# Two more token groups by seven products, three bands and statistics ahead, in a fused attention and convolution kernel

## The chip, the cores and the metric

The kernel runs on one core of a Trainium2 chip. The metric is the device time of one execution in microseconds. The engines are named as the profile names them: PE multiplies matrices, DVE, ACT and POOL work elementwise, and SP does nothing here but issue DMAs. Each engine takes its instructions in the order in which the kernel wrote them; instructions of different engines wait for each other by semaphores.

## The reference, cut to what matters

Two layers on an image batch x of shape (2, 56, 56, 384), all in float32. Layer 0 is neighbourhood attention and then an MLP; layer 1 is a projection to 768 channels, a 3x3 depthwise convolution, four exponential scans (both ways along rows and along columns), a projection back, and an MLP.

```python
# layer 0
x = x + neighborhood_attention(layer_norm(x), ...)            # result: x1
y = layer_norm(x, ln2_g, ln2_b)
x = x + (gelu(y @ w1 + b1) @ w2 + b2)                         # result: x2; w1 384x1536, w2 1536x384
# layer 1
p = _layernorm(x, n1_g, n1_b) @ w_in + b_in                   # 384 -> 768
local = conv_general_dilated(p, k_conv, ..., feature_group_count=768)   # 3x3 depthwise
lr, rl = _ema_scan(local, axis=2), _ema_scan(local, axis=2, reverse=True)
tb, bt = _ema_scan(local, axis=1), _ema_scan(local, axis=1, reverse=True)
mixed = _layernorm(0.25 * (lr + rl + tb + bt) + local, on_g, on_b)
x = x + (mixed @ w_out + b_out)
x = x + (gelu(_layernorm(x, n2_g, n2_b) @ w1 + b1) @ w2 + b2)
```

## The kernel before

**Stages.** The attention comes first (about the first 690 us). Its result x1 goes to DRAM (`x1f`). Then `passes` makes two passes over the 6272 tokens, in tiles of 128 tokens. The first pass runs the MLP of layer 0 and the projection to 768 channels; the second runs the projection back and the MLP of layer 1. Between them stands the convolution with its scans, which DVE computes beside the matrix products of both passes.

**Groups of the first pass.** `sizes` makes 13 groups: group 0 of one tile, groups 1 to 12 of four tiles (512 tokens). In each, group g's MLP runs (12 blocks of `hidden`, then `tokens`), and with it the previous group, held in `waiting`, is normalized and projected (`project_in`), which stores its 768 channels to DRAM as `p_d`. The next group's input `x_next` is loaded by SP (`load_group`, the tile `xa`) at the end of the group before. Its layer norm needs mean and variance per token: DVE takes them (`norm_next.add`: one bn_stats and one bn_aggr per tile), POOL takes the power -1/2, and ACT applies them.

**Groups by seven.** In the groups of `EARLY` (here 1 and 2) both MLP products are made from 2x2 blocks with seven block products in place of eight (`hidden_by_seven`, `tokens_by_seven`; L1580 and L1669 are their matmuls). Group `EARLY.stop` (here 3) is half early: `hidden` by seven, `tokens` plain. The early groups turn the next group's input on DVE (L1178), plain groups on PE (L269). The scratch tiles of the early groups lie in the pool `tp`, with one buffer per name. In the half early group `begin_convolution` frees that pool and opens the pool `cp` for the convolution in its place.

`hidden_by_seven` runs three rounds u = 0, 1, 2. In each round it calls `next(measuring)` twice, and there the generator `both()` puts in the work for the neighbouring groups, two of the twelve steps m for each call. I call these places slots: slot 1 and slot 2 of round u. In DVE's order the work of slot 2 stands in front of the addition L1627 of that round (PE's bank `z` plus the tile `u2`), and the work of slot 1 of round u + 1 stands between L1627 and the addition L1599 of round u (in `finish`). PE needs L1627 done before it adds to the same bank `z` in `finish`. ACT waits for L1599 with a gelu, and behind that gelu stands its copy L1619, which frees the bank that PE needs next.

**The convolution's plan.** `Beside` is a planner. Its jobs are `Band` (one band of image rows, one block of 128 channels: eight taps L1302, two scans L1248 and L1252) and `Columns` (the scans along columns). `BANDS` cuts the 56 rows of each image; a band is queued once `project_in` has covered its rows and the one below. After each piece of PE work the code calls `beside.go(worth, own)`: `worth` is the PE time by the planner's account (2.6 for one block `hidden`, 7.8 for one tile of `tokens`), `own` the DVE time of the group's own statistics, and DVE work of `rate * worth - own` is written out. `rate` is 1.06, and 0.98 from the last group on. Before the last group, `beside.until((0, NI - 1))` writes out whatever is left of image 0. In groups from `EARLY.stop` on, DVE takes the statistics of `x_next` at step m = 2, and those of `waiting`'s last tile at step m = 1.

Of the kernel before, what the change touches and what calls it, by code (L numbers as in the profile page):

```python
# [42 lines left out]
P = 128  # L43
# [4 lines left out]
NT = 4  # L48
# [15 lines left out]
    ((0, 19), (19, 28), (28, 37), (37, 47), (47, 56)),  # L64
# [49 lines left out]
class Beside:  # L114
# [3 lines left out]
    def __init__(self):  # L118
        self.jobs, self.due, self.finished, self.idle = [], 0.0, set(), True
        self.late, self.rate = [], 1.06  # L120
        self.steps = self.run()
# [38 lines left out]
    def go(self, worth, own=0.0):  # L160
        self.due += self.rate * worth - own
        while self.due > 0.0:
            step = self.step()
            if step is None:
                self.due = 0.0
            else:
                self.due -= step
# [9 lines left out]
def block_kernel(ctx: ExitStack, tc: tile.TileContext, ins: dict, out: bass.AP):  # L177
# [464 lines left out]
    EARLY = range(1, 3)  # L642
# [449 lines left out]
    def passes(xs, xn, w1, w2, between=lambda ps: None):  # L1092
# [164 lines left out]
        class Band:  # L1257
# [6 lines left out]
            def load(self):  # L1264
# [4 lines left out]
                self.pt = half("pt", "in")  # L1269
# [53 lines left out]
        class Columns:  # L1323
# [9 lines left out]
            def load(self):  # L1333
                if not self.loaded:
                    self.loaded = True
                    self.loc = [half("loc", "in") for h in range(2)]
                    for h in range(2):
                        nc.sync.dma_start(out=flat(self.loc[h]), in_=self.rows(loc_d, h))
# [163 lines left out]
        def project_in(g, hT, between=lambda: None, at=1):  # L1502
# [15 lines left out]
            while bands and bands[0][0] * T1 + min(bands[0][2] + 1, H) * W <= t0 + groups[g][1] * P:  # L1518
                b, lo, hi = bands.pop(0)
                last = [j for j in beside.jobs if isinstance(j, Columns) and not j.loaded][-2:]  # L1520
                beside.jobs = [j for j in beside.jobs if j not in last]
                beside.jobs += [Band(b, m, lo, hi) for m in range(NI)] + last
                if hi == H:
                    beside.jobs += [Columns(b, m) for m in range(NI)]

# [201 lines left out]

        ln2, n1 = ("L0_conv_ln2_g", "L0_conv_ln2_b"), ("L1_conv_n1_g", "L1_conv_n1_b")
# [8 lines left out]
        for g, (t0, n) in enumerate(groups):  # L1737
            def begin_convolution():
# [6 lines left out]
                decay = flat(decay)  # L1745
                ps_y = bctx.enter_context(tc.tile_pool(name="psy", bufs=1, space=PSUM))
# [9 lines left out]
            if g == last:  # L1756
# [3 lines left out]
                beside.rate = 0.98  # L1760
            if g < last:
                x_next, n_next = xs.pop(g + 1), groups[g + 1][1]
                norm_next = Norm(sm)
# [22 lines left out]
            def behind(m):  # L1786

                nonlocal xn_next
                if g < last:
# [7 lines left out]
                    if g >= EARLY.stop and m == 2:  # L1797
                        for k in range(n_next):
                            norm_next.add(k, [x_next[:, k, :]])
                        norm_next.close_by_pool(n_next)  # L1800
# [8 lines left out]
            def both():  # L1809
                for m in range(NHID):  # L1810
# [4 lines left out]
                    if m % 2 == 1:  # L1815
                        yield
# [23 lines left out]
            else:  # L1840
                for m in range(NHID):
# [6 lines left out]
                    own = STATS if m == 1 else n * STATS if m == 2 else 0.0  # L1848
# [260 lines left out]
```

## Time and profile before

| what | us |
|---|---|
| three runs | 2565.36, 2565.64, 2573.49; median 2565.64 |
| the profiled execution, its own time | 2573.64 |
| its span, first to last instruction | 2571.8 |
| PE busy in the span | 2545.4 |
| DVE busy in the span | 1973.7 |
| group 2 (by seven), first matmul 758.54 to the next group's 832.55 | 74.01 |
| group 3 (half early), from 832.55 | 79.76 |
| group 4 (with the preparation of w_out), from 912.31 | 85.54 |
| groups 5, 6, 7, ... (plain), from 997.85 | 79.93 or 79.94 each |
| first pass ends (group 12's tokens) | about 1639 |

The span is cut at the first matmul of each group's `hidden`. Start times are microseconds from the span's start. A row of the timeline gives start, duration, engine, line, operation, the tile written and those read, shapes, and in brackets how long the engine sat idle before it and what ended that. A matmul in float32 stands as two rows. "SPq" is SP issuing a DMA. In a table of windows, "busy (x)" is busy time and the number of instructions.

### The profile page before, as it was taken

Reading aid. Unit: us, or ns where it says so; the run is one execution under the profiler, and the core shown is the slowest. Engines: PE = TensorE matmul, PEld = TensorE weight load, DVE = VectorE, ACT = ScalarE, POOL = GpSimd, SP = SyncE. Lnnn points to the kernel's source line nnn. Section 1 sums busy time; section 2 is a strip of 40 time slices with the busy share of each in tenths; the row PEclk is TensorE's granted clock in tenths of the full one; section 3 lists DMA queues with packets and bytes.
Section 4 is the critical chain, followed back from the end, with each engine's and each line's share of the span. In section 5 each row is a group of like instructions: output and inputs, shape, how many; then the busy total and the mean of one; then the engine's idle time right before and its main releaser. Section 6 shows DMA issues by size and latency. Waiting matters only on the chain. (4 is left out here: it accounts for less than half of the span.)

```text
span 2571.8 us, 41605 instructions
## 1 busy us (share of the span) xinstructions
PE 2545.4 (99%) x16438; PEld 1695.7 (66%) x16438; DVE 1973.7 (77%) x3785; ACT 1115.9 (43%) x2030; POOL 560.9 (22%) x610
## 2 busy tenths in 40 slices
PE   9999999999999999999999999999999999999999
PEld 5666666666688645554455555555568888888888
DVE  3888878887544299967999958988887877878861
ACT  4656555555333444344454443333762233233222
POOL 0111111111443011101110011011123333333332
PEclk9999999999999999999999999999999999999999
DMA  6432454225511256655675655777781333333210
GB/s 210 161 100 87 151 190 153 88 85 191 158 43 38 79 147 173 167 132 149 178 273 191 183 174 162 239 208 191 187 213 24 74 74 74 74 74 74 47 28 21
DMA packets 162159, 338.50 MB, mean 132 GB/s; under 512 B 12086, under 2 KB 113952, under 8 KB 159648
## 3 DMA queue, kind: packets, MB, share of 16 engines
q1 hardware_dynamic: 128064, 251.18, 29.1%
q0 software_dynamic: 28944, 57.81, 13.7%
q10 hardware_dynamic: 4944, 26.74, 3.1%
q8 instruction: 131, 2.15, 0.3%
q14 instruction: 76, 0.62, 0.1%
HBM read 171.91 MB, written 134.88 MB: 119 GB/s over the span
## 5 line engine op out<-in xcount | busy, mean ns | idle before, releaser
L1302 DVE SCALAR_TENSOR_TENSOR loc<-pt,taps,loc 128x495 f32<-128x495 f32 (+13 forms) x432 | 397.8, 921 | 25.2 <-ACT loc L1285 9.4
L1195 PE MATMUL mm<-hT,w 128*128 128x512 f32 x864 | 378.6, 593 | 0.6 <-ACT hT L272 0.6
L1195 PEld LDWEIGHTS mm<-hT,w 128*128 128x128 f32 x864 | 161.6, 190 | 193.8 <-issue 185.2
L571 ACT ACTIVATE pts<-pts 119x448 f32<-119x448 f32 (+5 forms) x396 | 210.8, 573 | 110.4 <-DVE pts L561 101.5
L561 DVE TENSOR_TENSOR pts<-sc,bias 119x448 f32<-119x448 f32 (+5 forms) x396 | 219.0, 615 | 45.7 <-PE sc L550 45.4
L1213 PE MATMUL y<-w,hid 128*128 128x384 f32 x648 | 213.6, 486 | 0.2 <-ACT y L1223 0.2
L1213 PE MATMUL y_end<-w,hid 128*128 128x384 f32 x648 | 213.4, 486 | 0.0
L404 PE MATMUL ps<-hT,wqkv 128*128 128x448 f32 x504 | 207.7, 557 | 2.1 <-ACT vs L449 1.5
L1448 DVE STREAM_TRANSPOSE turned<-mx 32x192 f32<-32x192 f32 x528 | 194.8, 369 | 6.9
L1178 DVE STREAM_TRANSPOSE hT<-xn 32x96 f32<-32x96 f32 x656 | 176.8, 270 | 26.0 <-ACT xn L255 17.6
L1206 ACT ACTIVATE hid<-mm,chan 128x512 f32<-128x512 f32 x144 | 98.5, 686 | 185.4 <-PE mm L1195 185.4
L1213 PEld LDWEIGHTS y_end<-w,hid 128*128 128x128 f32 x648 | 122.7, 190 | 84.5
L1213 PEld LDWEIGHTS y<-w,hid 128*128 128x128 f32 x648 | 122.3, 190 | 84.3 <-ACT y L1223 0.8
L1195 PE MATMUL mm<-hT,w_in 128*128 128x512 f32 x396 | 171.9, 593 | 0.6 <-DVE hid_u L1599 0.6
L404 PEld LDWEIGHTS ps<-hT,wqkv 128*128 128x128 f32 x504 | 92.5, 192 | 86.1 <-issue 76.0
L1195 PEld LDWEIGHTS mm<-hT,w_in 128*128 128x128 f32 x396 | 75.1, 190 | 94.9 <-issue 88.8
L1321 POOL DMA_DIRECT2D mix_d<-both x54 | 52.2, 966 | 350.6 <-ACT both L1317 213.4
L227 POOL TENSOR_TENSOR rs<-rs,mhalf 128x4 f32<-128x4 f32 (+4 forms) x56 | 53.8, 960 | 331.1 <-DVE rs L224 321.2
L550 PEld LDWEIGHTS sc<-qT,kT 32*100 32x100 f32 (+3 forms) x3168 | 87.8, 169 | 46.4 <-DVE sum L580 7.6
L590 PE MATMUL o<-pts,vt 100*32 100x112 f32 (+3 forms) x3168 | 116.6, 264 | 0.8 <-ACT pts L571 0.8
L620 PE MATMUL ps<-wproj,og 128*128 128x384 f32 x294 | 107.0, 504 | 2.8 <-DVE og L533 2.1
L550 PE MATMUL sc<-qT,kT 32*100 32x112 f32 (+3 forms) x3168 | 106.5, 268 | 3.1 <-DVE pts L561 3.1
(197 smaller groups left out, 4649.5 us busy)
## 6 DMA issues: line engine op xcount, KB each, us to landing
loc<-loc_d SPq DMA_DIRECT2D x24, 784.0 KB
xa<-x_d SPq DMA_DIRECT2D x24, 768.0 KB
xa<-rows POOLq DMA_DIRECT2D x24, 768.0 KB, 8.6
bias<-in_bias_t ACTq DMA_DIRECT2D x13, 1344.0 KB
p_d<-mx SPq DMA_DIRECT2D x11, 1536.0 KB
mx<-mix_d SPq DMA_DIRECT2D x11, 1536.0 KB
v_d<-vs SPq DMA_DIRECT2D x49, 192.0 KB
xr<-in_x SPq DMA_DIRECT2D x49, 192.0 KB
```

What stands on the lines that cost most here:

```text
L404: nc.tensor.matmul(ps, lhsT=wqkv[:, c, m * P : (m + 1) * P], rhs=hT[:, c, half_of(n)], start=c == 0, stop=c == NC - 1,)
L550: nc.tensor.matmul(sc[i // 2][: w.keys, i % 2, q : q + TT], lhsT=kT[d, hg, w.keys_at + r * w.kc : w.keys_at + (r + w.rows) * w.kc], rhs=qT ...
L561: nc.vector.tensor_tensor(self.pts[:n, h : h + 2, lo:hi, :], sc[half][:n, :, at * TT : (at + hi - lo) * TT].rearrange("p h (c q) -> p h c ...
L571: nc.scalar.activation(t, t, AF.Exp)
L590: nc.tensor.matmul(o[i * HD : (i + 1) * HD, self.slot, :TT], lhsT=w.vt[:n, c, h * HD : (h + 1) * HD], rhs=self.pts[:n, i, c, :], start=c = ...
L620: nc.tensor.matmul(ps, lhsT=ogs[t // 7][:, c, at : at + P], rhs=wproj[:, c, :], start=c == 0, stop=c == NC - 1,)
L1178: nc.vector.transpose(hT[j : j + HD, :, k * P + i : k * P + i + HD], xn[i : i + HD, k, :].rearrange("p (c q) -> p c q", c=NC)[:, :, j : j ...
L1195: nc.tensor.matmul(ps[:, : n * P], lhsT=w[:, c, m * P : (m + 1) * P], rhs=hT[:, c, : n * P], start=c == 0, stop=c == NC - 1,)
L1206: nc.scalar.activation(t[:, : n * P], ps[:, : n * P], AF.Gelu, bias=col(b1, m))
L1213: nc.tensor.matmul(ps, lhsT=t[:, k * P : (k + 1) * P], rhs=w[:, m, :], start=m == 0 and onto is None, stop=m == len(lhs) - 1, skip_group_c ...
L1302: nc.vector.scalar_tensor_tensor(to, pt[:, lo + dy - self.top : hi + dy - self.top, xt : xt + n], self.tap(dy, dx), to, ALU.mult, ALU.add,)
L1448: nc.vector.transpose(t[j : j + HD].rearrange("p (m c) -> p m c", m=NI)[:, :, i : i + HD], mx[i : i + HD, :, k * P + j : k * P + j + HD],)
```

## The change

Groups 3 and 4 join groups 1 and 2 in `EARLY`; the half early group is now group 5. The convolution therefore begins in group 5, and `begun` keeps the planner from writing out bands before that. The first image has three bands in place of five, and the tiles `pt` and column `loc` get one line more. The planner's list is first in, first out: the lines that kept the last two `Columns` behind newly queued bands are gone. The rates are 1.07 and 1.0.

The statistics of x1 for groups 6 to 12 (28 tiles) are taken in the early groups: the generator `statistics_ahead` loads two tiles at a time into one tile `ahead` of the pool `tp`, and at its next call takes two bn_stats and two bn_aggr of it and issues the next load. It is called at the end of every slot of `both()` for g > 1, so at most six times in a group. After the last pair one DVE instruction, one POOL power of 128x28 and one DVE instruction make scale and shift for all 28 tiles. Groups from `EARLY.stop` on use them through `Ready` and take no statistics of `x_next`.

```diff
 BANDS = (
-    ((0, 19), (19, 28), (28, 37), (37, 47), (47, 56)),
+    ((0, 28), (28, 47), (47, 56)),
     ((0, 18), (18, 36), (36, 45), (45, 56)),
 )
...
-        self.late, self.rate = [], 1.06
+        self.late, self.rate, self.begun = [], 1.07, False
...
     def go(self, worth, own=0.0):
+        if not self.begun:
+            return
         self.due += self.rate * worth - own
...
-    EARLY = range(1, 3)
+    EARLY = range(1, 5)
...
-                last = [j for j in beside.jobs if isinstance(j, Columns) and not j.loaded][-2:]
-                beside.jobs = [j for j in beside.jobs if j not in last]
-                beside.jobs += [Band(b, m, lo, hi) for m in range(NI)] + last
+                beside.jobs += [Band(b, m, lo, hi) for m in range(NI)]
...
+        class Ready(Norm):
+            def __init__(self, g):
+                at = groups[g][0] // P - ready_from
+                self.rs, self.sh = (t[:, at : at + NT] for t in (ready_rs, ready_sh))
+
+        ready_from = groups[EARLY.stop + 1][0] // P
+        n_ready = T2 // P - ready_from
...
+        def statistics_ahead():
+            for k in range(0, n_ready, 2):
+                t = tp.tile([P, 2, C], F32, name="ahead")
+                at = (ready_from + k) * P
+                nc.sync.dma_start(
+                    out=t, in_=x1f[at : at + 2 * P, :].rearrange("(k p) c -> p k c", p=P)
+                )
+                yield
+                for i in range(2):
+                    st = sm.tile([P, 2, 6], F32, name="st")
+                    nc.vector.bn_stats(st[:, 0, :], t[:, i, :])
+                    nc.vector.bn_aggr(ready_mv[:, k + i, :], st[:, :1, :])
+            nc.vector.tensor_scalar(ready_rs, ready_mv[:, :, 1], EPS, 1.0, ALU.add, ALU.mult)
+            nc.gpsimd.tensor_tensor(
+                ready_rs, ready_rs, mhalf[:, :1].to_broadcast([P, n_ready]), ALU.pow
+            )
+            yield
+            nc.vector.scalar_tensor_tensor(
+                ready_sh, ready_mv[:, :, 0], -1.0, ready_rs, ALU.mult, ALU.mult
+            )
...
+                beside.begun = True
...
-                beside.rate = 0.98
+                beside.rate = 1.0
             if g < last:
                 x_next, n_next = xs.pop(g + 1), groups[g + 1][1]
-                norm_next = Norm(sm)
+                norm_next = Norm(sm) if g < EARLY.stop else Ready(g + 1)
...
-                    if g >= EARLY.stop and m == 2:
-                        for k in range(n_next):
-                            norm_next.add(k, [x_next[:, k, :]])
-                        norm_next.close_by_pool(n_next)
...
                     if m % 2 == 1:
+                        if g > 1:
+                            next(statistics, None)
                         yield
...
-                    own = STATS if m == 1 else n * STATS if m == 2 else 0.0
+                    own = STATS if m == 1 else 0.0
```

More of the change, by code (lines that the diff above doesn't have):

```diff
@@ L1268, in load @@
                 self.top, end = max(self.lo - 1, 0), min(self.hi + 1, H)
-                self.pt = half("pt", "in")
+                self.pt = cp.tile([P, HALF + 1, W], F32, name="pt", tag="in")
                 nc.sync.dma_start(
@@ L1335, in load @@
                     self.loaded = True
-                    self.loc = [half("loc", "in") for h in range(2)]
+                    self.loc = [
+                        cp.tile([P, HALF + 1, W], F32, name="loc", tag="in")[:, :HALF] for h in range(2)
+                    ]
                     for h in range(2):
@@ L1519, in project_in @@
                 b, lo, hi = bands.pop(0)
-                last = [j for j in beside.jobs if isinstance(j, Columns) and not j.loaded][-2:]
-                beside.jobs = [j for j in beside.jobs if j not in last]
-                beside.jobs += [Band(b, m, lo, hi) for m in range(NI)] + last
+                beside.jobs += [Band(b, m, lo, hi) for m in range(NI)]
                 if hi == H:
                     beside.jobs += [Columns(b, m) for m in range(NI)]
+        class Ready(Norm):
[4 more added lines that the diff above has]
+        n_ready = T2 // P - ready_from
+        ready_mv = wp.tile([P, n_ready, 2], F32, name="ready_mv")
+        ready_rs, ready_sh = (wp.tile([P, n_ready], F32, name=x) for x in ("ready_rs", "ready_sh"))
+        def statistics_ahead():
[18 more added lines that the diff above has]
+            )
         def store_x2(g, x2):
@@ L1726, in open_banks @@
             return ps_y, ps_u, bank_b, banks_b
+        statistics = statistics_ahead()
         ln2, n1 = ("L0_conv_ln2_g", "L0_conv_ln2_b"), ("L1_conv_n1_g", "L1_conv_n1_b")
```

## The prediction

> **What bounds the kernel now.** I read the page first, then a table of windows cut at the groups of the first pass, then the timeline of the first round of an early group, then the waits by length. The page:
>
> ```profile
> PE 2545.4 (99%) x16438; PEld 1695.7 (66%) x16438; DVE 1973.7 (77%) x3785; ACT 1115.9 (43%) x2030; POOL 560.9 (22%) x610
> ...
> PE   9999999999999999999999999999999999999999
> ```
>
> PE is never free, so an instruction less on PE shortens the run by its duration and a wait of PE lengthens it by its length. What the groups cost shows in the windows (length, then busy time of PE, PEld, DVE, ACT, POOL):
>
> ```profile
> 758.54:832.55 74.01, 73.18 (x350) 60.26 (x349) 29.93 (x95) 29.28 (x56) 22.59 (x23) 1.00 0.19 54
> 832.55:912.31 79.76, 78.46 (x292) 52.64 (x291) 30.89 (x45) 31.93 (x61) 5.16 (x6) 1.00 0.31 95
> 912.31:997.85 85.54, 85.54 (x241) 41.30 (x240) 80.68 (x80) 34.99 (x51) 12.55 (x10) 1.00 0.62 165
> 997.85:1077.79 79.94, 79.94 (x230) 41.29 (x229) 74.79 (x112) 33.73 (x55) 12.56 (x13) 1.00 0.64 160
> 1397.53:1477.46 79.93, 79.93 (x229) 41.28 (x228) 77.79 (x77) 34.61 (x50) 9.36 (x9) 1.00 0.59 167
> ```
>
> These are groups 2 (by seven), 3 (half early), 4, 5 and 10 (plain). The plain groups have PE busy throughout. The early group is shorter, but its PE lacks 0.8 us. The timeline shows why, in the first round of group 3, which starts at 832.55:
>
> ```profile
> 833.98 0.36 SPq L648 DMA_DIRECT2D xa<-x_d  x1
> ...
> 839.25 0.56 DVE L219 BATCH_NORM_STATS2 st<-xa 128x6 f32<-128x384 f32 x1 [3.67 <-DMA xa<-x_d]
> ...
> 840.60 0.53 DVE L219 BATCH_NORM_STATS2 st<-xa 128x6 f32<-128x384 f32 x1
> ...
> 842.27 0.68 DVE L1627 TENSOR_TENSOR hid_u<-uz,hid_u 128x512 f32<-128x512 f32 x1
> ...
> 843.09 1.10 PE L1580 MATMUL uz<-xsums,w 128*128 128x256 f32 x4 [0.75 <-DVE hid_u L1627]
> ...
> 845.10 0.69 DVE L1599 TENSOR_TENSOR hid_u<-uz,hid_u 128x512 f32<-128x512 f32 x1 [2.15 <-PE uz L1580]
> ...
> 846.64 0.56 ACT L1619 COPY hid_u<-ub 128x512 f32<-128x512 f32 x1
> ...
> 847.49 1.03 PE L1580 MATMUL ub<-xsums,w_t 128*128 128x256 f32 x4
> ```
>
> DVE waits for xa, takes four statistics (one pair from 839.25 to 840.60: 1.35 us), and only then makes L1627, for which PE waits 0.75 us. Group 2 shows the same, 0.78 us. Next, L1599 starts 2.01 us after that matmul; over a gelu and L1619, which ends at 847.20, it frees the bank that PE takes at 847.49: 0.29 us of slack. So in an early group DVE has no slack in slot 1 and slot 2 of round 0, though it is busy for 40% only.
>
> **What the Trainium skill says.** "DMA: Bandwidth & Descriptors", section on the anatomy of one DMA, fits a DMA as about 2.0 us plus bytes over 436e3 per us, mostly completion; for the 384 KB of one `ahead` load I estimate 2.0 + 0.9 = 2.9 us. That fit is for DMAs that GpSimd issues, ours are SP's. The trace has neighbours:
>
> ```profile
> 299.25 0.33 SPq L609 DMA_DIRECT2D xr<-in_x  x1
> ...
> 301.90 1.00 POOL L614 TENSOR_TENSOR xr<-xr,shift 128x384 f32<-128x384 f32 x1 [3.26 <-DMA xr<-in_x]
> ```
>
> 192 KB are usable 2.65 us after the issue, and 280 KB of `pt` 2.83 us (1211.45 to 1214.28). The 768 KB of xa took 5.27 us beside an equal store. I take 3.0 us for 384 KB. "Perfetto Trace Analysis", section Sequencer Loop, says that an engine's instruction waits for its semaphores in its queue; the trace agrees: the idle DVE leaves L1627 undone while the statistics in front wait for xa. "TensorE: Matmul & The Clock Gate", section on what's happening, puts the clock at half after an idle window of some 3.4 us; the windows above show 1.00 throughout, so no run here shows it yet.
>
> **The change part by part.** *Groups 3 to 6.* Before: 79.76 + 85.54 + 79.94 + 79.93 = 325.2 us. After: groups 3 and 4 as group 2, 2 x 74.01; group 5 half early, 79.76 less 0.75 (it takes no statistics of xa any more, so that wait goes); group 6 with the preparation of w_out, 85.54. Sum 312.6: **12.6 us less**.
>
> *Statistics ahead.* The order in which the changed kernel's instructions stand puts, on DVE, two bn_stats and two bn_aggr of `ahead` in front of L1627 and two more in front of L1599, in every round of groups 2 and 3 but for the very first slot, and up to the third slot of group 4; on SP each `ahead` load waits for DVE, since there is one tile. One slot is thus a trip: load 3.0 us (DVE to SP takes 0.03), pair 1.35. Two trips are 8.8 us, and a round of PE is 9.5, so in steady state they fit. The start of a group doesn't. Group 3, from its start:
> - xa at about 6.1 (before 6.7; the store of x2 now stands behind four loads on SP), four statistics and the small operations 2.85: 8.95.
> - Slot 1: pair (loaded long before), 10.3. Then the load, 13.3.
> - Slot 2: pair, 14.65; L1627, and PE's matmul 0.82 after it (842.27 to 843.09): 15.5, where it was 10.54. **Extra 4.95.**
> - Slot 1 of round 1: load 14.7 to 17.7, pair to 19.05. L1599 would start at 15.5 + 2.01 = 17.5. Late by 1.55, less the slack of 0.29: **extra 1.25.**
> - Slot 1 of round 2: the x2 store shares the wires with the load, about one us; **extra 0.2.**
>
> Group 3: 6.4. Group 4 the same without the last: its third slot ends the 28 tiles, 0.2 for the small operation: 6.3. Group 2: its first slot only loads, so slot 2 adds one pair less 0.15 for what lies between, 1.2; then again 1.2 and 0.2: 2.6. Sum **15.3 us of new waits**. With a load of 2.6 us the sum is about 13, with 3.4 about 18.
>
> *POOL's power of 128x28.* Four columns took 1.0 us (L227). Between 1.0 and, if it goes by columns, 7 us. Its result is wanted by a DVE instruction in front of L1627 of round 1, with about 6 us to spare: I take 0, at most 1.
>
> *PE's clock.* Groups 3 and 4 each get an idle stretch of about 6 us. At worst each costs a window at half speed, 1.7 us; much of it would fall on work that the late L1599 holds up anyway. Taken 0.5, range 0 to 3.
>
> *The convolution in fewer groups.* It had groups 3 to 12, now it has 5 to 12. Adding up what the planner hands out when each kernel is built: before group 12 it has written out 600 us (of its own account) in the old order and 531 in the new, `until` finds nothing left in either, and the queue of bands is then the same. So the plan closes; fewer bands save fixed costs, and the new plan is never empty, where before DVE stood idle 87.4 us for `pt`:
>
> ```profile
> DVE loc L1287 <- DMA pt<-p_d: 87.4, 5, 26.1
> ```
>
> What is to be shown is that DVE keeps the plan. In groups 8 to 10 it was full: 230 us of account took about 224 without the statistics (three windows of 79.93, less 3 x 6.5, plus the 3.7 by which it fell behind), so 0.974 real for one accounted. New: 481 accounted in groups 6 to 11, 468; statistics of x2, 6 x 2.9; w_out 4: 490 us against PE's 6 x 79.93 + 5.6 = 485. DVE falls behind by about 5 us, 1 per group, from 4.5 after group 6's start to about 10 at group 12. How far it was behind there:
>
> ```profile
> 1563.74 0.55 DVE L219 BATCH_NORM_STATS2 st<-xc 128x6 f32<-128x384 f32 x1
> ```
>
> 6.3 us after the group's start 1557.40. The first wait that ends on it is in group 12: PE's second transposes (1573.5) reuse banks that DVE's statistics of the first free (done about 1570.0), 3.9 us of slack. So some 4 more cost about 0.5. Through the planner's new 1.0 the last group of the second pass adds up to 1 to its present wait of 1.7. **Taken 1.5, range 0 to 10.** The longer bands move as many bytes in fewer DMAs, and the prefetch of `pt` is one job ahead: nothing. Fourteen issues on SP of 0.36 us: nothing, SP is idle there. The statistics that leave groups 6 to 12 take no PE time.
>
> Sum: -12.6 + 15.3 + 0.5 + 1.5 = **+4.7 us**. Against the profiled execution's own 2573.6 that is 2578.3; it lies 8.0 above the median of the runs, so on the median 2565.64 it is **2570.3 us**.
>
> **The rivals.** *The trips are hidden.* If the loads land before DVE comes to them, a pair costs only itself: 1.2 in group 2, and 2 x 1.35 less the earlier xa, 2.1, in groups 3 and 4: 5.4 us, and -7.2 in all with nothing for clock and lag, 2558.4. For it: DVE is busy 40% there, xr came in 2.65. Against: one tile, and a load that waits for the pair before.
>
> *DVE loses the plan.* Slower. If DVE falls behind by 2.6 us per group, as it did in group 9 (7.4 us after the start against 4.8 a group earlier), it is 20 behind at group 12, 14 more than before; less the slack of 3.9, PE waits 10 us at the statistics of the mixed rows. Then +13, 2579. It decides from 1.7 per group, where the sum passes +7.7. For it: 80 us of account per group without a pause. Against: group 10, as full, fell behind by 1.1 only.
>
> **How the numbers follow.** The measurement can't tell 0.3% (7.7 us) from no change. Likeliest case 0.60 (2563 to 2577, of which a fifth passes +7.7), hidden trips 0.15, the lost plan 0.25. Faster by over 0.3%: the hidden trips lie at that edge, 0.10 of their 0.15; slower: 0.25 and 0.12 of the likeliest (0.37); within: 0.53. The range 2558 to 2581 takes in the bounds of the waits (13 to 18), the clock and the lag.
>
> **What would show it.** Groups 3 and 4 of the changed profile should last about 80 us, not 74: PE idle about 5.7 us before the z matmul of round 0, ended by L1627's successor, with DVE idle on a DMA of `ahead`; and 1.3 us before the bank of round 1. Group 2 about 76.6, group 5 about 79.0. The last tile's statistic should start about 10 us after group 12's start. I am wrong if groups 3 and 4 last 74 to 76, or if PE waits for DVE in groups 6 to 12.

## The result, and the profile after

The changed kernel takes 2590.92 us (median of five runs, 2588.57 to 2593.11) against 2567.36 us of the kernel before on the same chip: a ratio of 1.0089, 95% interval 1.0074 to 1.0104. It is slower by 23.6 us, and 9.9 us above the end of the range. The profiled execution took 2590.42 us, its span is 2588.6 us.

The page of after, engines and PE's row of the slices:

```profile
PE 2538.1 (98%) x16676; PEld 1736.5 (67%) x16678; DVE 1993.0 (77%) x3783; ACT 1127.4 (44%) x2046; POOL 566.9 (22%) x621
...
PE   9999999999999999999999998999999999999999
```

PE did get less to do (2538.1 us busy, 2545.4 before), but the span grew by 16.8 us. So PE waits more, or runs more slowly, and the page can't tell where. The windows can tell. They are cut as before, at the first matmul of each group's `hidden`: length, busy time of PE, PEld, DVE, ACT, POOL, then PE's granted clock, DMA share and GB/s. Of after:

```profile
750.82:826.67 75.85, 73.45 (x351) 60.26 (x349) 36.45 (x115) 29.45 (x56) 22.59 (x23) 1.00 0.28 84
826.67:908.29 81.62, 75.98 (x349) 62.22 (x349) 37.90 (x119) 29.53 (x56) 22.61 (x23) 0.96 0.27 78
908.29:989.98 81.69, 76.22 (x351) 62.40 (x350) 35.13 (x109) 29.41 (x56) 27.36 (x24) 0.96 0.20 59
989.98:1068.74 78.76, 78.21 (x291) 52.71 (x291) 46.30 (x41) 33.85 (x62) 3.93 (x4) 1.00 0.37 112
1068.74:1154.61 85.87, 85.81 (x241) 41.22 (x240) 80.13 (x55) 35.38 (x48) 6.14 (x7) 1.00 0.72 199
1314.48:1400.23 85.75, 82.12 (x230) 41.90 (x228) 74.49 (x56) 45.70 (x70) 8.03 (x5) 0.98 0.75 257
1560.20:1687.21 127.01, 120.03 (x349) 62.78 (x347) 113.82 (x130) 44.66 (x67) 15.53 (x15) 0.96 0.73 217
```

These are groups 2, 3, 4, 5, 6, 9 and 12. Groups 2 and 3 are longer by 1.8 and 1.9 us, group 4 shorter by 3.9, group 5 by 1.2; group 6 now carries the preparation of w_out that group 4 carried before. Up to there, groups 2 to 6 together are 4.6 us longer, where I had worked out 3.2. The loss stands in two groups that the change seemed hardly to touch: group 9 (79.94 before) and group 12 (115.87 before), with 5.8 and 11.1 us. Of before, the same two groups:

```profile
1317.59:1397.53 79.94, 79.94 (x230) 41.28 (x229) 74.55 (x57) 40.09 (x61) 8.68 (x5) 1.00 0.65 224
1557.40:1673.27 115.87, 115.23 (x349) 60.89 (x347) 103.09 (x121) 45.26 (x68) 16.34 (x13) 1.00 0.69 206
```

In after PE idles 3.6 us in group 9 and is busy 2.2 us longer than before; in group 12 it idles 6.3 us more and is busy 4.8 us longer. The granted clock is below 1.00 in these two windows: 4.8 of group 12's 11.1 us are slow matmuls, not waits.

The attention stage, the same code in all these kernels, ended anywhere from 666.7 to 676.9 us after the span's start in the profiled executions, and was 7.8 us shorter in the profiled run of after than in that of before. From here on I compare the *passes*: from the first `hidden` of group 0 to the first matmul of the last group of the second pass. They took 1874.95 us before and 1899.38 after, 24.4 more, which agrees with the 23.6 of the medians.

### The profile page after: what moved, and what is told of

It is laid out like the page before. It is cut to its first block, busy times and chain, and to the rows that moved or that the text cites. A ratio compares the mean times of both kernels' runs of the same rounds, so it can differ in the third digit from the quotient of the medians.

```text
span 2588.6 us, 42020 instructions
## 1 busy us (share of the span) xinstructions
PE 2538.1 (98%) x16676; PEld 1736.5 (67%) x16678; DVE 1993.0 (77%) x3783; ACT 1127.4 (44%) x2046; POOL 566.9 (22%) x621
## 5 line engine op out<-in xcount | busy, mean ns | idle before, releaser
L1304 DVE SCALAR_TENSOR_TENSOR loc<-pt,taps,loc 128x495 f32<-128x495 f32 (+12 forms) x336 | 377.1, 1122 | 24.7 <-ACT loc L1287 15.3
L1197 PE MATMUL mm<-hT,w 128*128 128x512 f32 x720 | 320.1, 599 | 3.7 <-ACT hid L1208 3.5
L1197 PEld LDWEIGHTS mm<-hT,w 128*128 128x128 f32 x720 | 135.9, 192 | 166.4 <-issue 155.9
L1180 DVE STREAM_TRANSPOSE hT<-xn 32x96 f32<-32x96 f32 x784 | 211.2, 269 | 27.7 <-ACT xn L257 17.5
L1452 DVE STREAM_TRANSPOSE turned<-mx 32x192 f32<-32x192 f32 x528 | 194.7, 369 | 10.5 <-issue 3.6
L1215 PE MATMUL y<-w,hid 128*128 128x384 f32 x552 | 183.7, 490 | 2.1 <-ACT y L1225 2.1
L1215 PE MATMUL y_end<-w,hid 128*128 128x384 f32 x552 | 181.8, 486 | 0.0
L1215 PEld LDWEIGHTS y_end<-w,hid 128*128 128x128 f32 x552 | 104.5, 190 | 71.8
L406 PEld LDWEIGHTS ps<-hT,wqkv 128*128 128x128 f32 x504 | 91.3, 189 | 84.4 <-issue 74.2
L1197 PE MATMUL mm<-hT,w_in 128*128 128x512 f32 x324 | 140.8, 593 | 0.6 <-DVE hid_u L1635 0.6
L1616 PE MATMUL ua<-hT,w 128*128 128x256 f32 x504 | 123.1, 380 | 0.0
L1623 ACT ACTIVATE hid<-hid_u,chan 128x256 f32<-128x256 f32 x168 | 76.1, 500 | 96.7 <-DVE hid_u L1635 71.8
L592 PE MATMUL o<-pts,vt 100*32 100x112 f32 (+3 forms) x3168 | 115.9, 263 | 0.4 <-ACT pts L573 0.4
```

Of the source, the lines that this page charges most:

```text
L406: nc.tensor.matmul(ps, lhsT=wqkv[:, c, m * P : (m + 1) * P], rhs=hT[:, c, half_of(n)], start=c == 0, stop=c == NC - 1,)
L592: nc.tensor.matmul(o[i * HD : (i + 1) * HD, self.slot, :TT], lhsT=w.vt[:n, c, h * HD : (h + 1) * HD], rhs=self.pts[:n, i, c, :], start=c = ...
L1180: nc.vector.transpose(hT[j : j + HD, :, k * P + i : k * P + i + HD], xn[i : i + HD, k, :].rearrange("p (c q) -> p c q", c=NC)[:, :, j : j ...
L1197: nc.tensor.matmul(ps[:, : n * P], lhsT=w[:, c, m * P : (m + 1) * P], rhs=hT[:, c, : n * P], start=c == 0, stop=c == NC - 1,)
L1215: nc.tensor.matmul(ps, lhsT=t[:, k * P : (k + 1) * P], rhs=w[:, m, :], start=m == 0 and onto is None, stop=m == len(lhs) - 1, skip_group_c ...
L1304: nc.vector.scalar_tensor_tensor(to, pt[:, lo + dy - self.top : hi + dy - self.top, xt : xt + n], self.tap(dy, dx), to, ALU.mult, ALU.add,)
```

## The experiments

Four theories on where groups 9 and 12 lose their time were tried. T1: DVE is given more work per group than it does in the time of one, falls behind, and the engines that wait for it in order hold up PE. T2: the order of the jobs, now that Columns are not held back. T3: the longer bands. T4, formed on the way: an add of the last band that gets stuck in POOL's queue. A table of all runs first, lengths in us from the windows of each profile ("d2" is the last dense group of the second pass, "tail" the half group behind it):

| kernel | g2 | g3 | g4 | g6 | g9 | g12 | d2 | tail | passes | one run |
|---|---|---|---|---|---|---|---|---|---|---|
| before | 74.0 | 79.8 | 85.5 | 79.9 | 79.9 | 115.9 | 84.3 | 31.6 | 1875.0 | 2573.6 |
| after | 75.9 | 81.6 | 81.7 | 85.9 | 85.8 | 127.0 | 84.9 | 33.7 | 1899.4 | 2590.4 |
| e1_rates | 75.8 | 80.6 | 81.1 | 85.5 | 79.9 | 122.3 | 103.4 | 40.0 | 1911.5 | 2608.9 |
| late_slots | 73.1 | 73.2 | 73.1 | 85.9 | 86.4 | 123.9 | 84.9 | 33.0 | 1876.6 | 2565.9 |
| hold | 75.7 | 80.6 | 81.1 | 85.9 | 85.2 | 127.3 | 86.0 | 34.7 | 1899.7 | 2598.1 |
| five_bands | 75.9 | 80.6 | 81.2 | 85.5 | 84.0 | 118.1 | 106.2 | 38.9 | 1916.4 | 2608.3 |
| light | 75.9 | 80.3 | 81.1 | 85.9 | 84.4 | 115.9 | 84.9 | 32.5 | 1883.7 | 2583.2 |
| three_a | 75.9 | 77.1 | 78.8 | 79.9 | 90.4 | 115.7 | 92.4 | 35.3 | 1895.6 | 2591.1 |
| no_ahead | 73.9 | 75.0 | 73.7 | 85.6 | 79.9 | 125.3 | 98.9 | 38.8 | 1894.7 | 2585.9 |
| soon | 75.9 | 80.6 | 80.9 | 85.9 | 80.9 | 124.3 | 84.7 | 32.8 | 1888.7 | 2579.0 |
| late_soon | 73.2 | 73.5 | 73.0 | 85.9 | 81.1 | 121.8 | 85.1 | 33.7 | 1870.0 | 2562.6 |
| three_b | 73.1 | 74.4 | 78.9 | 79.9 | 80.2 | 116.2 | 84.0 | 31.6 | 1868.0 | 2557.3 |
| three_b5 | 73.1 | 74.4 | 78.9 | 79.9 | 80.2 | 116.2 | 83.5 | 31.6 | 1867.4 | 2557.5 |
| late_12 | 73.2 | 73.2 | 73.1 | 85.9 | 80.4 | 125.8 | 91.5 | 32.9 | 1879.0 | 2573.0 |

In three_a, three_b and three_b5 group 4 is the half early one and group 5 has the preparation of w_out.

### The statistics moved out of the first round (late_slots)

```diff
-                        if g > 1:
+                        if m > 3:
                             next(statistics, None)
```

Here m counts the twelve steps of a group. The condition takes the first round out, and lets group 1 take part.

> The kernel after, with the statistics ahead called only from the slots of the second and third round of the hidden layer (step 5 and later of 12), in groups 1 to 4. If the waits for the statistics' loads in the first round are what makes groups 3 and 4 81.6 us long (idle of 5.6 and 5.4 us before the z product, then a slow clock), both fall to 75.5 to 77.5 us and group 2 from 75.9 to 74 to 75.5, together 9 to 12 us less; groups 6 to 12 stay within 1.5 us each. If the statistics cost VectorE the same wherever they stand, the wait goes to a later round and the three groups lose less than 3 us.

The timeline of after in the first round of group 3, around the place the prediction had named:

```profile
836.22 0.53 DVE L1551 BATCH_NORM_STATS2 st<-ahead 128x6 f32<-128x384 f32 x1
836.77 0.36 SPq L1545 DMA_DIRECT2D ahead<-x_d  x1
839.89 0.56 DVE L1551 BATCH_NORM_STATS2 st<-ahead 128x6 f32<-128x384 f32 x1 [2.88 <-DMA ahead<-x_d]
...
841.24 0.66 DVE L1663 TENSOR_TENSOR hid_u<-uz,hid_u 128x512 f32<-128x512 f32 x1
...
842.05 2.04 PE L1616 MATMUL uz<-xsums,w 128*128 128x256 f32 x4 [5.59 <-DVE sh L250]
```

DVE finishes a pair, SP issues the next load, 3.12 us after that issue DVE takes the first statistic of the next pair, and only behind that pair comes the addition L1663 that PE waits for. (The releaser named is a small instruction of DVE that ends last before PE starts; L1663 ends at 841.90.) PE idles 5.59 us, and then the four matmuls take 2.04 us.

Without statistics in that round, late_slots has in the same place:

```profile
831.03 0.68 DVE L1663 TENSOR_TENSOR hid_u<-uz,hid_u 128x512 f32<-128x512 f32 x1
...
831.86 1.10 PE L1616 MATMUL uz<-xsums,w 128*128 128x256 f32 x4
```

and its windows of groups 2, 3 and 4 are

```profile
749.01:822.08 73.07, 73.03 (x350) 60.31 (x349) 35.31 (x111) 29.29 (x56) 22.60 (x23) 1.00 0.26 76
822.08:895.30 73.22, 73.18 (x350) 60.30 (x349) 35.32 (x111) 29.29 (x56) 22.61 (x23) 1.00 0.26 76
895.30:968.37 73.07, 73.02 (x351) 60.30 (x349) 35.29 (x109) 29.29 (x56) 27.29 (x24) 1.00 0.23 65
```

No wait, no slow clock, the same 28 statistics, and 19.8 us less in the three groups, where 9 to 12 were expected. So it was their place in the first round that cost, not the statistics. In group 3 of after, 5.6 us are idle PE (81.62 less 75.98) and 2.8 us are PE's own slower work (75.98 against 73.18). The second part is the clock: in the trace of after it stands at 0.50 from 842.05 to 847.72, where PE is busy throughout. The Trainium skill, "TensorE: Matmul & The Clock Gate", section What's actually happening, says that the PE's clock falls to half after an idle window of some 3.4 us and comes back after one of work; the trace agrees after this idle of 5.59 us, 2.04 against 1.10 us for the same four matmuls. A wait of only 2.12 us, in group 9 below, was followed by half clock too; there the measurement decides.

Group 12 came down by 3.1 us too, where at most 1.5 was expected. The last tile's statistic of x2, the fourth, stands 14.6 us after the group's start as in after, so DVE is as late in both; but 1.7 of the 3.1 us are matmuls at full instead of half clock (PE busy 118.34 against 120.03). A group with a long wait can so differ by a few us between two runs with the same lag.

### No statistics ahead at all (no_ahead)

```diff
-                norm_next = Norm(sm) if g < EARLY.stop else Ready(g + 1)
+                norm_next = Norm(sm)
...
+                    if g >= EARLY.stop and m == 2:
+                        for k in range(n_next):
+                            norm_next.add(k, [x_next[:, k, :]])
+                        norm_next.close_by_pool(n_next)
...
-                        if g > 1:
-                            next(statistics, None)
...
-                    own = STATS if m == 1 else 0.0
+                    own = STATS if m == 1 else n * STATS if m == 2 else 0.0
```

> The kernel after without the statistics ahead: VectorE takes them in the dense groups as in before, and the planner counts them there. The early groups lose the waits for the statistics' loads: groups 2, 3 and 4 at 73 to 74.5 us each, some 18 us less in sum than after if the waits and the slow clock behind them are the whole of it. T1: the dense groups have some 7 us less each for the convolution, the planner's account leaves 15 us for the last dense group of the second pass, which grows by 25 to 35 us together with the half group behind it; groups 9 and 12 as in after or a little shorter; in sum 0 to 15 us slower than after. Rival (the statistics cost VectorE nothing in the dense groups, since it waits there anyway): no growth at the end, and some 18 us faster than after.

Groups 2 to 4 became 16.7 us shorter, and d2 with the tail grew by 19.2 where 25 to 35 was expected; group 9 came down to 79.9, which was not expected, so that the passes are 4.7 us shorter than in after instead of up to 15 longer. The statistics ahead are needed: without them DVE's work of the convolution comes back where PE waits for it.

### Less written out per group (e1_rates)

```diff
-        self.late, self.rate, self.begun = [], 1.07, False
+        self.late, self.rate, self.begun = [], 1.03, False
...
-                beside.rate = 1.0
+                beside.rate = 1.02
```

> The kernel after, with only the two rates of the convolution's planner lowered (1.07 to 1.03, 1.0 to 1.02), so that less of VectorE's convolution is written out beside each dense group. T1 (VectorE is given more per group than it does in the group's 79.9 us, falls behind, and ScalarE's in-order waits on it hold up TensorE): group 9 falls from 85.8 to about 80 us and group 12 from 127.0 to 116 to 118; some 11 us of the planner's own account are then left for the last dense group of the second pass, which gets 5 to 8 us longer; in sum 8 to 12 us faster than after. T2 (the order of the Columns jobs, no longer held back, is the cause, not the amount): groups 9 and 12 keep their extra 5.8 and 11.1 us, and the whole stays within 3 us of after or gets longer by what is left over.

The first rate holds up to group 11; from group 12 on a little more is written out than in after. Group 9 did fall to 79.9, group 12 only to 122.3, and d2 and the tail grew by 18.5 and 6.3 us, for 11 us of account left over: 12.1 us slower over the passes, where 8 to 12 faster were expected. The two longest waits of PE in the second half of e1_rates (us in total, times, longest), the second of them in group 12:

```profile
PE yb L1229 <- ACT hT L274: 9.2, 1, 9.2
PE xi L1440 <- DMA mx<-mix_d: 4.0, 1, 4.0
```

PE waits 9.2 us at the end of d2 and 3.5 us in the tail behind it (L1616, for DVE); in front of both `until` has DVE finish the columns that are left. With the rates alone the work only moves, and at the end it costs more than it is counted. That group 9 healed seemed to speak for T1, since DVE was less late there too, but the rates had also moved where in group 9 the bands of the first image end. The runs light and soon, below, part the two.

### The order of the jobs, and the bands (hold, five_bands)

```diff
-                beside.jobs += [Band(b, m, lo, hi) for m in range(NI)]
+                last = [j for j in beside.jobs if isinstance(j, Columns) and not j.loaded][-2:]
+                beside.jobs = [j for j in beside.jobs if j not in last]
+                beside.jobs += [Band(b, m, lo, hi) for m in range(NI)] + last
```

> The kernel after, with the two last unloaded Columns jobs again held back behind each new band. T2 (the order is the cause of the lag): groups 9 and 12 lose most of their extra 5.8 and 11.1 us and the whole is about 15 us faster than after. T1 (the amount is the cause): the same account is written out by the same groups, the lag comes back at the same or a neighbouring group, and groups 6 to 12 together keep at least 15 of their extra 23 us over before.

Nothing changes: 85.2 and 127.3 us in groups 9 and 12, 1899.7 over the passes. T2, in the form of the order of Columns, falls.

```diff
-    ((0, 28), (28, 47), (47, 56)),
+    ((0, 19), (19, 28), (28, 37), (37, 47), (47, 56)),
```

> The kernel after, with the first image cut in the five bands of before again. T3 (the longer bands are the cause: each of their operations keeps VectorE longer before ScalarE's turn): groups 6, 9 and 12 fall back to 80, 80 and 116 us, and what more there is to write out (26 us of the planner's account left for the last dense group of the second pass) comes back there as 10 to 20 us. T1: the planner writes the same 80 us a group, so the lag and at least two of the three long groups stay, and the last dense group of the second pass is longer besides; slower than after by 5 to 20 us.

Group 9 is still 84.0 and d2 is 106.2: 17 us slower over the passes, so three bands are a gain of the change. (Group 6 could not fall to 80 as T3 had it; it carries the preparation of w_out.) The run decides less on T3 than I expected. Groups 7 and 8 grew as well, by 0.6 and 2.6 us, and in groups 8 and 9 PE waits 1.8 and 2.2 us for the normalized x2 (L271 for L257), while the stall that is found below for group 9 of after is not there: SP waits 10.1 us where it waits 29.2 in after. So group 9 is long for another reason here, and whether the three bands brought that stall about is not shown. Group 12, at 118.1, is nearly well again; what counts there is shown below.

### DVE lighter, the plan unchanged (light)

This kernel leaves out one of the eight taps; everything else keeps its order.

```diff
-                        nc.vector.scalar_tensor_tensor(
-                            to, pt[:, lo + dy - self.top : hi + dy - self.top, xt : xt + n],
-                            self.tap(dy, dx), to, ALU.mult, ALU.add,
-                        )
+                        if not (dy == 1 and dx == 1):
+                            nc.vector.scalar_tensor_tensor(
+                                to, pt[:, lo + dy - self.top : hi + dy - self.top, xt : xt + n],
+                                self.tap(dy, dx), to, ALU.mult, ALU.add,
+                            )
                         yield us(self.n)
```

> The kernel after, with one of the eight taps that VectorE adds to each band (the lower right one) left out of the convolution, while the planner still counts it: the same jobs in the same order and groups, but 42 VectorE instructions of 1.1 us, some 4 us a dense group, are not run. T1 (VectorE is given more than it does in a group): groups 9 and 12 fall to 80 to 81 and 116 to 118 us, the last dense group of the second pass and the first half group behind it stay at or below 85 and 33 us; 15 to 20 us faster than after. T2 (the order of the jobs and of ScalarE's and SyncE's waits, not VectorE's amount): the order is unchanged, and at least 10 of the extra 17 us of groups 9 and 12 stay.

This run split the loss in two. Group 12 fell to 115.85, all of its 11.1 us: there T1 holds. Group 9 kept 4.4 of its 5.8 us (84.35, where 80 to 81 was expected), although DVE was no longer late there (it took the fourth statistic of x2, the last tile's, 6.7 us after the group's start, in after 15.6): for these 4.4 us T1 falls. The 1.4 that went are about PE's wait for the normalized x2, 1.5 us in after and 0.2 here.

**Group 12** is a chain from a late DVE. The timeline of after:

```profile
1564.62 0.32 SPq L1272 DMA_DIRECT2D pt<-p_d  x1
1567.28 1.14 SPq L1427 DMA_DIRECT2D mx<-mix_d  x1
1569.94 1.04 ACT L1319 ACTIVATE both<-both 128x1008 f32<-128x1008 f32 x1 [9.05 <-DVE both L1254]
1571.61 4.39 PE L1197 MATMUL mm<-hT,w 128*128 128x512 f32 x6 [3.52 <-ACT hid L1208]
...
1579.33 1.51 PE L1440 MATMUL xi<-ident,mx 128*128 128x128 f32 x6 [3.33 <-DMA mx<-mix_d]
```

and, with DVE about 9 us earlier against the group's start (which is 1565.3 there, 1560.2 in after), light:

```profile
1560.76 0.32 SPq L1272 DMA_DIRECT2D pt<-p_d  x1
1562.84 0.50 SPq L1428 DMA_DIRECT2D mx<-mix_d  x1
...
1576.06 0.85 PE L1441 MATMUL xi<-ident,mx 128*128 128x128 f32 x6 [0.29 <-DMA mx<-mix_d]
```

SP's waits of after, from 1068 to 1700 us (us in total, times, longest):

```profile
SPq L1272 <- DVE loc L1304: 307.0, 28, 21.8
```

SP can load the next band `pt` only when DVE is through with an old one; behind it in SP's queue stands the load of the mixed rows, which PE needs at the start of the second pass. So DVE's lag passes through SP's queue to PE: 3.33 us. ACT in the same way stands 9.05 us before L1319, which waits for DVE's scan, with the gelus that PE needs behind it: 3.52 us. The load's wait ends last, and it is what counts: in soon and late_soon, below, PE waits for the load alone (5.8 and 4.6 us), and group 12 is still long. Behind it the clock is at half for a while: the six transposes of 1579.33 take 1.51 us, in light 0.85.

Over all runs the length of group 12 goes with the time at which SP issues this load, more than with the fourth statistic. Issued 2.5 to 6.7 us before the group's start (before, light, three_a, three_b, three_b5) it leaves the group at 115.7 to 116.2 us; 0.9 before (five_bands), 118.1; 2.8 to 8.4 after it (the eight others), 121.8 to 127.3. In e1_rates the fourth statistic is hardly later than in before, 7.1 us against 6.3, and the group is 122.3; in five_bands it is 10.6.

### The end of the bands against the group (three_a, soon)

three_a gives the planner one dense group more: four lines, `EARLY = range(1, 4)`, rates 1.02 and 0.98, and `if m > 1:` for the statistics.

> Three groups by seven block products rather than four (groups 1 to 3, with group 4 half early), statistics ahead from step 3 on in each of them, rates 1.02 and 0.98: the planner has one dense group more, about 80 us of VectorE, for the same convolution and ends with nothing left over. T1: no group lags; groups 2 and 3 at 73 to 75 us, group 4 near 79, group 5 near 86, groups 6 to 11 within 0.5 us of 80, group 12 at 116 to 118, the last dense group of the second pass at 84 to 86 and the half group behind it at 31.6 to 32.5; both passes together some 1865 to 1870 us against 1875 in before and 1877 in late_slots. T2 (what makes groups 9 and 12 long is an order of waits that comes with the new bands, whatever the amount): groups 9 and 12 or two like them keep 5 and 8 us or more, and the passes take at least 1878 us.

Group 12 fell to 115.7 as T1 has it, but group 9 rose to 90.4, though DVE was given less and its fourth statistic stood 8.8 us after the group's start. (d2 and the tail were longer than expected too, 92.4 and 35.3.) So group 9 needed another cause. SP's waits of after have it, the longest single one from 1200 to 1420 us (us in total, times, longest):

```profile
SPq L1381 <- DMA mix_d<-both: 29.2, 1, 29.2
```

The timeline of after, group 9, only the instructions concerned:

```profile
1330.23 0.41 SPq L1381 DMA_DIRECT2D mixed<-mix_d  x1
...
1331.14 4.14 POOL L238 TENSOR_TENSOR rs<-rs,mhalf 128x4 f32<-128x4 f32 x1 [13.97 <-DVE off L237]
...
1336.15 0.71 ACT L257 ACTIVATE xn<-xc,sh,rs 128x384 f32<-128x384 f32 x1 [5.33 <-POOL sh L239]
...
1342.10 0.64 ACT L1319 ACTIVATE both<-both 128x504 f32<-128x504 f32 x1
...
1351.17 1.35 POOL L1136 DMA_DIRECT2D xa<-rows  x1 [15.06 <-ACT xn L257]
...
1352.00 1.45 POOL L1323 DMA_DIRECT2D mix_d<-both  x1
...
1359.92 0.32 SPq L1381 DMA_DIRECT2D mixed<-mix_d  x1
...
1382.95 3.60 PE L1215 MATMUL y<-w,hid 128*128 128x384 f32 x6 [2.12 <-ACT y L1225]
```

The last band of the first image ends just before group 9. Its sum has to be added to the mix by POOL (L1323), and the planner issues that add 11 of its steps later. Among bands such steps are short; among Columns, which come next, they are long (a scan takes 1.2 us in that band and 3.4 in Columns), so the add falls behind POOL's work for group 9: the power, which waits for DVE, and the transfer into xa, which waits 15 us for ACT. The add is issued at 1352.00, and the second half of the second Columns job can be loaded only then (1359.92). By the code's rotation of four buffers that load wants the buffer which the add reads; this I read from the code and the releaser, and did not test apart. POOL's row of 1.45 us is not the transfer: the Trainium skill, "Perfetto Trace Analysis", section DMA Instruction — SWDGE (GPSIMD), says that such a row ends when the descriptors are made and not when the data has moved, and the trace agrees, with the load released 7.9 us after the row's start. Behind it stand the loads of the next columns, behind these ACT's copies, and at 1382.95 PE, which waits 2.12 us and then runs at half clock: the clock is 0.50 from 1383.61 to 1387.02, and the 24 matmuls that start at 1382.95 take 9.70 us, 7.90 at full clock. To test that:

```diff
-                beside.later(lambda: nc.scalar.mul(flat(both), flat(both), share), 8)
-                beside.later(lambda: add_to_mix(self.b, self.m, at, both), 11)
+                soon = self.b == 0 and self.hi == H and self.m == NI - 1
+                beside.later(lambda: nc.scalar.mul(flat(both), flat(both), share), 2 if soon else 8)
+                beside.later(lambda: add_to_mix(self.b, self.m, at, both), 3 if soon else 11)
```

> The kernel after, with one thing moved: for the last band of the first image (the last channel block, rows 47 to 56) ScalarE's scaling and GpSimd's add to the mix are issued 2 and 3 of the planner's steps later rather than 8 and 11. T4 (group 9's stall is one of order on GpSimd: the add stands behind the power of the group's statistic, which waits for VectorE, and behind the transfer of the x rows, which waits for ScalarE; the first Columns jobs wait for the add's buffer, 29 us, and with them SyncE's loads): group 9 falls from 85.8 to 80 to 81 us, group 12 and the rest as in after, within 1.5 us of 127. T1 (VectorE's amount): the stall stays or comes one group later, and groups 9 to 11 together keep at least 4 us of the extra 5.9.

soon's timeline and SP's waits in the same stretch:

```profile
1328.53 4.14 POOL L238 TENSOR_TENSOR rs<-rs,mhalf 128x4 f32<-128x4 f32 x1 [13.44 <-DVE off L237]
1332.74 0.74 POOL L239 TENSOR_TENSOR sh<-off,rs 128x4 f32<-128x4 f32 x1
1333.43 0.90 POOL L1324 DMA_DIRECT2D mix_d<-both  x1
```

```profile
SPq L1382 <- DMA mix_d<-both: 9.2, 1, 9.2
```

The add is still behind the power, but ahead of the transfer into xa; SP waits 9.2 us and not 29.2, and group 9 takes 80.85 us. The same DVE work in the same order, one band's add moved, with the scaling on ACT that it needs: T4 holds for 4.9 of the 5.8 us. DVE's fourth statistic stands 15.3 us after the group's start, as late as in after (15.6), so it wasn't the lag. The other runs agree: SP waits 9.0 to 15.4 us for this add where group 9 takes 79.9 to 81.1 us (before, no_ahead, e1_rates, soon, late_soon, three_b5, late_12), and 28.0 to 35.0 where it takes 84.4 to 90.4 (after, late_slots, hold, light, three_a); five_bands is the exception named above. In no_ahead the fourth statistic stands 13.5 us after group 9's start, and nothing is lost.

Group 12 came down by 2.7 us as well, which was not expected. Without the stall the fourth statistic stands 10.5 us after the start there and not 14.6, and the load of mx is issued 2.8 us after the group's start and not 7.1; 1.7 us of the difference are clock (PE busy 118.34 against 120.03).

### Putting it together (late_soon, three_b, three_b5, late_12)

> late_slots with the earlier add: groups 2 to 4 at 73 us each as in late_slots, group 9 at 80 to 81 (T4), group 12 between 118 and 127; both passes together some 1868 to 1874 us against 1875 of before, 1877 of late_slots and 1899 of after. If T4 falls: 1875 to 1879.

As expected: 1870.0 us over the passes, group 9 at 81.1, group 12 at 121.8.

three_b is three_a without the statistics of the first round, with group 5's statistics taken in group 4 and the earlier add:

```diff
-    EARLY = range(1, 5)
+    EARLY = range(1, 4)
...
-        ready_from = groups[EARLY.stop + 1][0] // P
+        ready_from = groups[EARLY.stop + 2][0] // P
...
-                norm_next = Norm(sm) if g < EARLY.stop else Ready(g + 1)
+                norm_next = Norm(sm) if g <= EARLY.stop else Ready(g + 1)
...
+                    if g == EARLY.stop and m == 2:
+                        for k in range(n_next):
+                            norm_next.add(k, [x_next[:, k, :]])
+                        norm_next.close_by_pool(n_next)
```

with rates 1.02 and 1.0, and the diffs of late_slots and soon.

> Three groups by seven block products (1 to 3, group 4 half early), statistics ahead only from step 5 on and for groups 6 to 12 (group 5's taken in group 4 as in before), rates 1.02 and 1.0, and the earlier add. T1 and T4 together: groups 2 and 3 at 73 to 73.5, group 4 near 79.5, group 5 near 85.7, groups 6 to 11 at 80, group 12 at 116 to 117, the last dense group of the second pass at 84 to 86; both passes together 1866 to 1870 us, which is 5 to 9 less than before. If group 9 keeps the 10 us it had in three_a, T4 is wrong and the passes take 1876 to 1880.

One run of 2557.31 us; passes 1868.0, as expected, with group 3 at 74.4 a little above. More runs of the same kernel:

> The kernel of three_b again, timed: the passes 5 to 9 us shorter than before's with an attention stage that varies by some 8 us from run to run, so a median of 2556 to 2564 us, 0.995 to 0.999 of before. If the 2557 of the single look came from a short attention stage alone: no difference from before.

2558.77 us against 2571.61 of before beside it: ratio 0.9951, 95% interval 0.9935 to 0.9967. It is 0.5% faster than before, a small gain but clear of the noise, and so faster than after. Its windows of groups 2, 3, 9 and 12:

```profile
750.22:823.29 73.07, 73.02 (x351) 60.27 (x349) 35.32 (x111) 29.29 (x56) 22.61 (x23) 1.00 0.26 76
823.29:897.65 74.36, 73.18 (x350) 60.26 (x349) 35.32 (x111) 29.28 (x56) 22.60 (x23) 1.00 0.26 75
1301.86:1382.06 80.20, 80.20 (x230) 41.20 (x229) 76.01 (x47) 44.83 (x68) 4.32 (x3) 1.00 0.73 255
1541.93:1658.13 116.20, 115.49 (x349) 60.80 (x347) 105.90 (x123) 45.25 (x68) 15.07 (x13) 1.00 0.73 221
```

The clock is full throughout; PE idles 1.2 us in group 3, 0.7 in group 12 and not in group 9. The last one asked which of the two waits makes group 12 long when four groups are kept: in late_soon, 8 and 11 steps become 12 and 15.

> late_soon with ScalarE's scaling and GpSimd's add of every other band 12 and 15 of the planner's steps late rather than 8 and 11. If ScalarE's wait for VectorE in front of the gelus (9.1 us in group 12 of after, 4.9 us in late_soon) is what lengthens group 12, it falls from 121.8 to 116 to 119 us and the passes take 1864 to 1868 us, as good as three_b or better. If it is the late load of the mix (the product xi waits 4.6 us for it in late_soon), behind SyncE's other issues, group 12 stays at 120 to 127 us and the passes at 1869 to 1876.

Group 12 took 125.8 us. The delay took little from ACT's wait (3.9 us, 4.9 in late_soon), so the run hardly tests it; but PE waits for nothing in group 12 except the load of mx, 7.3 us, and that fits the second case. SP issued the load as early as in late_soon (2.9 and 2.8 us after the group's start); it landed 14.9 us after its issue and not 12.2, and PE was busy 1.2 us longer at a slower clock. d2 grew too (91.5), with 5.2 us of PE's waiting for a gelu, and the passes came out longer than either case had it; ratio to before 1.0003 (0.9993 to 1.0013). A four-group version with group 12 cured was not found.

## Why the prediction was wrong

*Groups 3 to 6, -12.6.* Right. With the waits taken away (late_slots) groups 3 to 6 are 310.9 us against 325.2, 14.3 less; the rest of the difference is that the groups by seven then take 73.1 and not 74.0.

*Statistics ahead, +15.3, and the clock, +0.5.* Right in place, and nearly in sum by luck: against the 74.01 that I had started from, groups 2, 3 and 4 lost 1.84, 7.61 and 7.68, in all 17.1 for 15.8. The idle stretch was given as about 5.7 us and is 5.59 and 5.42. Two terms in it were off and nearly cancel. The 1.25 us at the bank of round 1 did not come in groups 3 and 4, where PE itself was slow by then; and the clock cost 2.8 us in group 3 and 3.0 in group 4 where I had 0.25 each, in sum outside the range of 0 to 3 that I gave it. I had argued that the slow matmuls would fall on time that is waited for anyway; they didn't. Nor was it so that no run had shown a slow clock: in the profile of before it stands at 0.50 from 637.93 to 644.70, in the attention stage, with PE busy for 5.2 of the 6.9 us in front of that. I had taken only the windows of the groups.

*POOL's power of 128x28, 0.* No wait of PE names POOL.

*The convolution in fewer groups, "Taken 1.5, range 0 to 10".* This is the step that failed. It cost 19.7 us: 5.8 in group 9, 0.1 in group 10, 11.1 in group 12, 0.7 in d2, 2.0 in the tail. DVE's lag was in part off: I had about 10 us at group 12; in after it is 14.6, and 10.5 in soon, where group 9's stall is away. What was wrong above all is the price of a lag, and that I took DVE for the only engine concerned. "The first wait that ends on it", with 3.9 us of slack, was to be PE's second transposes. In fact SP's queue came first: the load of mx stands behind a load that waits for DVE, and with a 10.5 us lag group 12 was 8.4 us longer (soon, 124.29 against 115.87), not 0.5: 5.3 us of idle PE and 3.1 of slow clock behind it, for which I had nothing in these groups. And I had asked only if the plan closes in sum, not where in a group the bands of the first image end; there the add waits on POOL, and it costs 4.4 us even with DVE on time (light).

The ratio of 0.974 real to one accounted was too kind too. The fourth statistic of x2 stands 6.4, 7.5, 10.3 and 15.6 us after the starts of groups 6, 7, 8 and 9 of after: DVE falls behind by 1.1, 2.7 and 5.3 us per group, where I had 1. Why the account misses there was not tried.

*The rivals.* "The trips are hidden" fell. "DVE loses the plan" had the right sign and the right group, but it too had the wait at PE's statistics, and its 2579 was 12 us short: it had nothing for group 9 and no more for the clock than I had. Of the signs I had named for being wrong, the second came: PE waits for a late DVE in group 12, though through SP and ACT, so that no line of PE's waits names DVE there.

The parts of the change, as far as the runs part them: the two groups more by seven give 14 us, the statistics ahead take back 17 to 20 only by their place, the three bands save 17 (against five_bands), and the convolution in fewer groups costs 19.7, of which 4.9 is the add on POOL (soon). What stays open: d2 and the tail of after, 2.7 us together, were seen to go (three_b5, 83.5 and 31.6) but not tried alone.

## What to carry to other kernels

When work is moved into fewer groups, a sum that closes is not enough: ask of each in-order queue (SP's loads, POOL's adds, ACT's copies) which instruction will stand behind one that waits for the engine that gets fuller, for here the lag reached the bound engine that way first. Count the slow clock behind a wait with the wait. A delay that is counted in steps is a different delay when the steps change their size. And before a piece of side work is judged too dear, move it by one slot: the 28 statistics cost 20 us when some of them stood in first rounds, and nothing in the second and third.

## What the runs showed of the hardware

- Behind a wait of PE of 5.4 to 5.9 us in groups 3 and 4, slow matmuls took 2.8 and 3.0 us more in after (75.98 and 76.22 us busy against 73.18, group 3 of late_slots), and 1.5 to 2.5 in e1_rates, hold, five_bands, light and soon, with the same kernel in these groups.
- The length of a wait alone didn't tell whether half clock follows. At 1382.95 in after a wait of 2.12 us, was followed by six matmuls in 3.60 us, where 24 of the kind take 7.90 at full clock; at 843.42 in three_a a wait of 2.47 us was followed by four matmuls in 1.10 us, full clock.
- PE, waiting for the load of mx, could start 12 to 15 us after its issue (12.05 in after, 12.22 in late_soon, 14.85 in late_12).
- POOL's power on 128x4 took from 1.03 to 4.14 us in one execution of after (median 2.06, eight of them), always the same shape; the slow one stood in group 9, in front of ACT's late normalization.
- A GpSimd add of 258 KB into DRAM was usable 4.35 us after its issue in soon (1333.43 to 1337.78) and 7.9 us in after.
